# Infinity row of a Winograd-style dynamic convolution taken by direct products from DRAM taps, with the first softmax's transposes among them

## The chip, the cores and the metric

The kernel runs on one core of a Trainium2 chip. The metric is the device time of one execution in microseconds (us). Before the change three runs took 764.07, 766.85 and 767.55 us; the median is 766.85 us. The engines are called PE (matrix products), ACT (activations and copies), DVE (vector operations), POOL (vector operations and DMA descriptors) and SP (DMA issue). Each runs its own list of instructions in order, and they meet through semaphores.

## The reference

The input x is (4, 256, 64, 64) in float32: four images of 256 channels. Layer 0 makes, for each pixel, 49 attention weights, and sums the 49 shifted neighbours (7x7, dilation 2) with them. Layer 1 whitens the result over groups of 64 channels. Cut to what matters:

```python
k = lax.conv_general_dilated(x, w1, (1, 1), [(6, 6), (6, 6)], rhs_dilation=(2, 2), dimension_numbers=DN) + b1
k = lax.conv_general_dilated(k, w2, (1, 1), [(0, 0), (0, 0)], dimension_numbers=DN) + b2
attn = softmax(k, axis=1)                      # 49 weights per pixel
y = einsum('bkchw,bkhw->bchw', shifts, attn)   # 49 shifted copies of x
# layer 1, g = 4 groups of 64 channels, over all pixels of all images
Sigma = EPS * I + einsum('gdm,gem->gde', xc, xc) / m
# five Newton steps for Sigma^(-1/2), then xn = wm @ xc, times weight plus bias
```

## The kernel before

**Weights and points.** The two convolutions are folded at the start into one 7x7 convolution with 49 outputs, whose taps lie in `tap`. It is computed by evaluation and interpolation in both directions (Winograd's scheme): seven points 1, -1, 0, 2, -2, infinity (`INF`, number 6) and 1/2 for rows, and the same for columns. For a row point br, `row_eval` combines rows of x into `rb`, `col_ops` evaluates the columns into seven tiles `xh`, `conv_bank` multiplies them on PE with the weights `wr` in three banks (`BANKS`: three, three and one column points), ACT copies each bank from PSUM (`cv`) to `pv`, and `col_interp` turns a row's seven columns into `zz[:, br]` on DVE. When all rows are there, `row_interp` gives the logits. The row of infinity needs only the products of one row of taps (`taps(INF)` is `(0,)`), so it has half of a row's products.

**Direct products.** `direct` computes a row point without evaluating columns: 7 column taps v times 2 halves of channels times 2 halves of rows, each a product of up to 512 columns. It is used for image 0's rows infinity, 0, 4 and 5 (`direct0`) and, at the end of image 0's stage, for image 1's infinity, with the taps in SBUF and the result in `acc`.

**Stages.** Image 0 is computed with everything in a fixed order on DVE (`strict`). Then for b = 1, 2, 3 a list of steps `(cost, f)` is run: `conv_step` of each row in `ROWS`, which for images 2 and 3 begins with infinity. Each step also prepares (`prepare`: weights, row and column evaluation) the same bank of the next row. After each eighth of the costs a `gap` is filled with work of the image before: `soft` (softmax over 49, transposes on PE, exponentials on ACT), and for each quarter n of an image `first_half` and `second_half`, in which PE transposes blocks of x (`make_block`), multiplies them with a band matrix of the attention weights (`weighted_sum`), ACT stores y (`store_y`), and PE gathers the moments for layer 1 (`turn_y`, `moments`). The band matrix comes from softmax over DRAM: ACT copies terms into `zt` (`move_terms`), SP stores them to `sd` and loads them skewed into `band` in three parts, and DVE transposes the blocks (`load_band`).

**Weights over DRAM.** Row weights of points 4 and 5 and of infinity are kept in DRAM (`kept`: `g4d`, `g5d`, `gi`). When a row is first used after image 0, `weights` loads them into `rb[0]`, makes the bank's column weights on DVE and ACT, and stores them to `gd`; later images only load them. Two or three of the copies in it, `o0[0]`, `o1[0]` and `o0[INF]`, are plain copies on ACT (lines 405, 406 and 415).

**Slots.** The halves of an image lie in five slots. `move` stores slots 0 to 2 to DRAM when their image is finished and loads image 2's second half and image 3 there, by POOL's DMA queue.

**Buffers.** `pv` has `NV` = 3 buffers that rotate by row; the scratch tile of `col_interp` for b > 0 is the last point of the buffer after the next. `pivot`, a bias for y, is a DVE reduction behind image 0's stage (line 812).

Of the kernel before, what the change touches and what calls it, by code (L numbers as in the profile page):

```python
# [11 lines left out]
ALU = mybir.AluOpType  # L12
# [13 lines left out]
BANKS = ((1, 2, 0), (3, 4, 6), (5,))  # L26
ORDER = sum(BANKS, ())

ROWS = (INF, 0, 1, 2, 3, 4, 5)


@with_exitstack
def kernel(
# [222 lines left out]
    zz = apool.tile([P, NP, Q9, W], F32, name="zz")  # L256
    nc.gpsimd.memset(zz[:, INF], 0.0)

    NV = 3
    pv = apool.tile([P, NV, NP, Q9, 2 * Q9], F32, name="pv")  # L260
    ct = apool.tile([P, Q8 * 4 * Q8, 4], F32, name="ct")
    rb = [apool.tile([P, Q8, 2, NCC, W], F32, name=f"rb{k}") for k in range(3)]
    xh = {}
# [11 lines left out]

    TT, STT = nc.vector.tensor_tensor, nc.vector.scalar_tensor_tensor

    turn, strict = [None], [False]

    def in_turn(ins):  # L280


        if turn[0] is not None:
            tc.add_manual_dep(
                ins.ins,
                turn[0],
                mybir.DependencyInfo(mybir.DependencyClass.NoSync, mybir.DependencyReason.DATA),
                reason="in_turn",
            )
        if strict[0]:  # L290
            turn[0] = ins.ins.name
        return ins

    @contextmanager
# [66 lines left out]
    def weights(b, br, i, mid=None):  # L361

        first = (br, i) not in made
        made.add((br, i))
        s0 = slot_of[BANKS[i][0]]
        ns = sum(len(taps(bc)) for bc in BANKS[i])  # L370
        nk = NSK * len(taps(br)) // 2
        wt = apool.tile([P, ns, NSK], F32, tag=f"wr{i}", name=f"wr_{b}_{br}_{i}")[:, :, :nk]
        w = {bc: wt[:, slot_of[bc] - s0 : slot_of[bc] - s0 + len(taps(bc))] for bc in BANKS[i]}
        if not first:
            nc.sync.dma_start(wt, gd[br][:, s0 : s0 + ns])
            return w

        if br == 0:
            g = [gr0[:, v] for v in range(KS)]
        elif br in kept:  # L380

            f = rb[0].rearrange("p q r c w -> p (q r c w)")[:, : KS * nk]
            if i == 0:
                nc.sync.dma_start(f, kept[br])
            f = f.rearrange("p (v a r k) -> p v a r k", v=KS, a=NCC, k=KT)
            g = [f[:, v] for v in range(KS)]
        else:
            g = [gbr[:, v] for v in range(KS)]
        g = [t.rearrange("p a r k -> p (a r k)") for t in g]

        e = ct.rearrange("p a b -> p (a b)") if b else store[4].rearrange("p c r w -> p (c r w)")
        e, o, e1 = (e[:, k * nk : (k + 1) * nk] for k in range(3))
        g0 = [g[KS - 1 - a] for a in range(4)]
        g1 = [g[KS - 5 - a] for a in range(3)]
        o0 = {bc: w[bc][:, 0] for bc in w}
        o1 = {bc: w[bc][:, 1] for bc in w if bc != INF}
        if i == 0:
            add(e, g0[0], g0[2])
            add(o, g0[1], g0[3])
            add(e1, g1[0], g1[2])  # L400
            add(o0[1], e, o)
            sub(o0[2], e, o)
            add(o1[1], e1, g1[1])
            sub(o1[2], e1, g1[1])
            nc.scalar.copy(o0[0], g0[0])
            nc.scalar.copy(o1[0], g1[0])
        elif i == 1:
            madd(e, g0[2], 4.0, g0[0])
            madd(o, g0[3], 4.0, g0[1])
            madd(e1, g1[2], 4.0, g1[0])  # L410
            madd(o0[3], o, 2.0, e)
            madd(o0[4], o, -2.0, e)
            madd(o1[3], g1[1], 2.0, e1)
            madd(o1[4], g1[1], -2.0, e1)
            nc.scalar.copy(o0[INF], g0[3])
        else:
            madd(o0[5], g0[0], 2.0, g0[1])
            madd(o1[5], g1[0], 4.0, g1[2])
            madd(o0[5], o0[5], 2.0, g0[2])
            if mid is not None:  # L420
                mid()
            madd(o1[5], g1[1], 2.0, o1[5])
            madd(o0[5], o0[5], 2.0, g0[3])
            add(o1[5], o1[5], o1[5])
        for bc in BANKS[i]:
            f = SCALE[bc] * (SCALE[br] if br not in kept else 1.0)
            if f != 1.0:
                nc.scalar.mul(w[bc], w[bc], f)
        nc.sync.dma_start(gd[br][:, s0 : s0 + ns], wt)
        return w  # L430
# [82 lines left out]
    def conv_bank(b, br, i, w):  # L513

        if i == 0:
            slot[b, br] = len(slot) % NV
        pts = BANKS[i]
        i0 = sum(len(k) for k in BANKS[:i])
        cv = cv_buf[ncv[0] % 2][:, : 3 * PT].rearrange(
# [34 lines left out]
                    reason="later",  # L554
                )

    def interpolate(pt, tmp, outs, cut, part=None):

        lo = lambda t: cut(t, 0)
        hi = lambda t: cut(t, 1)
        c0, s1, s2, s3, s4, hh, c6 = (pt[b] for b in (0, 1, 2, 3, 4, 5, 6))
        if part != 1:
            add(tmp, s1, s2)
            sub(s2, s1, s2)  # L570
            add(s1, s3, s4)
            sub(s4, s3, s4)
            add(s3, c0, c6)
            madd(s1, tmp, -2.0, s1)
            sub(s3, tmp, s3)
            madd(tmp, tmp, -30.5, s1)
            sub(s4, s4, s2)
            madd(tmp, s3, 22.5, tmp)
            madd(s1, c0, 1.5, s1)
            madd(tmp, s2, -16.0, tmp)  # L580
            madd(s1, c6, -30.0, s1)
            if part is None:
                add(tmp, tmp, s4)
            madd(s3, s1, -1.0 / 6, s3)
            madd(outs[0], lo(s1), 1.0 / 6, hi(c0))
            if part == 0:
                add(outs[2], lo(c6), hi(s3))
                add(s3, tmp, s4)
        if part != 0:
            madd(hh, tmp if part is None else s3, -1.0 / 9, hh)  # L590
            if part is None:
                add(outs[2], lo(c6), hi(s3))
            madd(s4, hh, -3.0, s4)
            sub(s2, s2, hh)
            madd(s2, s4, -1.0 / 15, s2)
            madd(outs[1], lo(s4), 1.0 / 15, hi(s2))
# [5 lines left out]
    def col_interp(b, br, part=None):  # L602
# [6 lines left out]
        }  # L609
        outs = phases(zz[:K2, br].rearrange("p q (w two) -> p q w two", two=2))  # L610
        cut = lambda t, k: t[:, :, k : k + Q8]
        if b > 0:

            t = pv[:K2, (at + 2) % NV, NP - 1].rearrange("p q b -> p (q b)")
        else:
            t = ct.rearrange("p a b -> p (a b)")[:K2, :PT]
        interpolate(
            pt, t.rearrange("p (q b two) -> p q b two", q=Q9, two=2), outs, cut, part
        )

        def end():
            ins = nc.scalar.copy(outs[3], cut(pt[5], 0))
            if br == INF:

                nc.gpsimd.memset(zz[:, INF, Q8], 0.0)
            return ins

        if part is None and b > 0 and br != ROWS[-2]:
# [22 lines left out]

    logits = {}

    def direct(b, br, s, ps, w, xr=None):


        a = 3 if br == INF else 0
        order = [(v, cc) for v in sorted(range(KS), key=lambda v: abs(v - R)) for cc in range(NCC)]
        for j, (v, cc) in enumerate(order):
            d = 2 * (v - R)  # L660
            w0, w1_ = max(0, -d), min(W, W - d)
            for h in range(2):
# [22 lines left out]
    def conv_psum():  # L685
        ncv[0] += 1
        return cv_buf[(ncv[0] - 1) % 2].rearrange("p (q w) -> p q w", w=W)

    acc = ps_y.tile([P, 2, Q8, W], F32, tag="y", name="acc")
    nc.vector.memset(acc, 0.0)  # L690
    rows = [(0, br) for br in (1, 2, 3)]
    NR0 = len(rows)
    rows += [(b, br) for b in range(1, B) for br in ROWS[1 if b == 1 else 0 :]]
    cur, nxt = {}, {}

    def prepare(k, i):

# [3 lines left out]
            cur["x"] = row_eval(b, br)  # L701
        nxt.update(w)
        col_eval(cur["x"], i)

    def conv_step(k, i):
        w = {bc: nxt.pop(bc) for bc in BANKS[i]}
# [54 lines left out]
    for i in three:  # L761
        bank(0, i)
        both0(xr, 2, i)
    for s in range(2, 4):
        load_x(s, s, nc.gpsimd)
    for i in three:
# [16 lines left out]
    for sr in range(2):  # L783
# [14 lines left out]
    prepare(NR0, 0)  # L798
    direct0(5, 1)
    row_interp(0, 1)  # L800

    direct(1, INF, 0, acc[:, 0], [tap[:, UPOS[3], v] for v in range(KS)])
    prepare(NR0, 1)
    prepare(NR0, 2)
    strict[0] = False
    gpool.release()

    npix = SH * W // 4  # L810
    in_turn(
        nc.vector.tensor_reduce(
            pivot, slots[0].rearrange("p a r w -> p a (r w)")[:, :, :npix], AX.X, ALU.add
        )
    )
    nc.vector.tensor_scalar(pivot, pivot, -1.0 / npix, None, ALU.mult)

# [116 lines left out]

    BAND = ((0, 3), (3, 5), (5, 8))

    def load_band(n, part):

        if (n, part) in loaded or n not in moved:
# [4 lines left out]
        for g in range(CR):  # L946
# [5 lines left out]
                    ap=[[DW - 1, SW], [KS * SW, m1 - m0], [1, KS * SW]],  # L952
                ),
            )
        f = band[:, m0:m1].rearrange("p m r w -> p (m r w)")
        with tc.high_priority():
            nc.vector.transpose(f, f)  # L957
        if (n, part) == (4 * B - 1, len(BAND) - 1):
            bring_back(dma)

# [231 lines left out]
    for b in range(1, B):  # L1192

        steps = []
        for k, (bk, br) in enumerate(rows):
            if bk == b:
                for i, cost in enumerate((6, 5, 2)):
                    steps.append(
                        (cost * len(taps(br)) / 2, lambda k=k, i=i: conv_step(k, i))
                    )  # L1200
        if b == 1:
            steps.insert(0, (0, lambda: soft(0, 0)))
            steps.insert(4, (0, lambda: soft(0, 1)))
        j, at, whole = 0, 0, sum(c for c, _ in steps)
        for cost, f in steps:
            f()
            at += cost
            if at * NPC >= (j + 1) * whole:
                gap(b, j)
# [220 lines left out]
```

## Time and profile before

| what | value |
|---|---|
| median of three runs | 766.85 us |
| the profiled execution | 761.8 us, of it a span of 760.0 us |
| granted TensorE clock, mean | 0.978 |
| PE, products of the banks (L531) | 4576 records, 268.8 us |
| PE, direct products (L668), image 1's infinity and those to `acc` | 168 records of `acc<-slot,tap`, 34.6 us |
| DVE, interpolation on pv (L310, L306), two largest groups | 327 instructions, 98.4 us |
| DVE, transposes of band (L957) | 48 instructions, 50.9 us |
| ACT, evictions of banks (L541) | 69 instructions, 33.2 us, 101.8 us of waiting before them |
| POOL | 45 instructions, 33.7 us |

A product in float32 appears as two records. Busy time of PE is the time covered by records; durations on DVE overlap a little with the next instruction, so that the starts of two neighbours lie closer together than the duration says.

### The profile page before, as it was taken

The page shows a single profiled execution, that of the slowest core. Times are in us where ns is not written, and L with a number is a line of the kernel's source. Part 1 is how long each engine was busy: PE and PEld are TensorE (multiplying, and loading weights), DVE is VectorE, ACT ScalarE, POOL GpSimd, SP SyncE. Part 2 cuts the span into 40 slices and gives each one's busy share as a digit, 9 for nine tenths or more (in the row PEclk, how much of TensorE's full clock was granted, in tenths as well). Part 3 has the DMA queues.
Part 4 walks back from the last instruction along what each step waited for, and adds up shares of the span by engine and source line. Part 5 has one row for each costly group of instructions (what it writes and reads, how often), then busy time and mean ns, then how long its engine had stood idle before and what let it go on. Part 6 is the DMA issues. An engine that isn't in the chain of part 4 may idle for free.

```text
span 760.0 us, 18845 instructions
## 1 busy us (share of the span) xinstructions
PE 698.6 (92%) x7608; PEld 539.3 (71%) x7608; DVE 643.0 (85%) x1394; ACT 342.8 (45%) x980; POOL 33.7 (4%) x45
## 2 busy tenths in 40 slices
PE   6999999996999877999999977999999889998996
PEld 1459643376998766888998967998898668885322
DVE  3799899999999989999994999999979675545665
ACT  1414240255355726366545442745435473322464
POOL 0410000020000010002000100000000000000000
PEclk9999999999899989999999998999999999999999
DMA  8981120227163563246745731342532134363488
GB/s 323 254 293 72 60 86 0 87 98 233 33 220 120 198 216 88 80 141 217 226 137 184 233 105 47 126 111 91 165 90 79 50 98 140 117 232 136 191 357 338
DMA packets 62911, 115.39 MB, mean 152 GB/s; under 512 B 26295, under 2 KB 45416, under 8 KB 62056
## 3 DMA queue, kind: packets, MB, share of 16 engines
q1 hardware_dynamic: 59128, 95.31, 38.4%
q0 software_dynamic: 3696, 18.88, 7.2%
q8 instruction: 60, 0.98, 0.6%
q14 instruction: 27, 0.22, 0.1%
HBM read 66.18 MB, written 47.98 MB: 150 GB/s over the span
## 4 chain that ended last, share of the span: by engine, by line
DVE 44%; PE 41%; ACT 5%; DMA 4%; issue 4%; SPq 1%; DVEq 0%; ACTq 0%
PE cv L531 9%; PE y L1004 8%; PE acc L668 6%; DVE xh L310 6%; DVE pv L310 5%; DVE rb L310 4%; PE tp L1370 4%; DVE ct L310 3%; DVE band L957 3%; DVE ct L303 3%; DVE zz L310 3%; DVE pv L306 2%; PE tp L1036 2%; PE tp L975 2%; PE sig L1057 2%
## 5 line engine op out<-in xcount | busy, mean ns | idle before, releaser
L531 PE MATMUL cv<-xh,wr 128*49 128x128 f32 (+1 forms) x4576 | 268.8, 279 | 19.5 <-issue 7.3
L531 PEld LDWEIGHTS cv<-xh,wr 128*49 128x49 f32 x4576 | 260.6, 126 | 25.5 <-issue 18.0
L1004 PE MATMUL y<-band,xb 128*128 128x224 f32 (+2 forms) x640 | 151.2, 374 | 15.0 <-ACT xb L983 12.9
L1004 PEld LDWEIGHTS y<-band,xb 128*128 128x128 f32 x640 | 109.6, 193 | 36.4 <-ACT xb L983 16.0
L541 ACT COPY pv<-cv 113x486 f32<-113x486 f32 (+1 forms) x69 | 33.2, 483 | 101.8 <-PE cv L531 101.5
L1023 ACT ACTIVATE slot<-y,pivot 128x512 f32<-128x512 f32 x53 | 36.8, 741 | 62.1 <-PE y L1004 62.1
L310 DVE SCALAR_TENSOR_TENSOR pv<-pv 113x162 f32<-113x162 f32 x215 | 63.8, 318 | 0.5
L1044 ACT COPY yt<-tp 128x256 f32<-128x256 f32 x128 | 45.9, 379 | 36.3 <-PE tp L1036 35.2
L957 DVE STREAM_TRANSPOSE band<-band 128x960 f32<-128x960 f32 (+1 forms) x48 | 50.9, 1060 | 9.9 <-DMA band<-sd 9.9
L1036 PE MATMUL tp<-ident,slot 128*128 128x128 f32 x256 | 52.0, 299 | 4.4 <-ACT yt L1044 2.3
L975 PE MATMUL tp<-ident,slot 128*128 128x128 f32 x256 | 50.5, 300 | 4.6 <-ACT yt L1044 4.5
L1036 PEld LDWEIGHTS tp<-ident,slot 128*128 128x128 f32 x256 | 41.3, 205 | 13.3 <-issue 3.2
L975 PEld LDWEIGHTS tp<-ident,slot 128*128 128x128 f32 x256 | 40.4, 206 | 11.0 <-ACT yt L1044 6.0
L906 ACT COPY zt<-d 32x112 f32<-32x112 f32 (+2 forms) x156 | 45.0, 289 | 1.8
L860 ACT ACTIVATE d<-tp,mx 128x49 f32<-128x49 f32 x128 | 37.5, 335 | 14.0 <-DVE mx L855 10.7
L310 DVE SCALAR_TENSOR_TENSOR xh<-ct 128x512 f32<-128x512 f32 x46 | 30.3, 683 | 10.2 <-PE cv L531 10.2
L1057 PE MATMUL sig<-yt 128*64 128x65 f32 x1024 | 36.9, 225 | 0.0
L1057 PEld LDWEIGHTS sig<-yt 128*64 128x64 f32 x1024 | 32.5, 137 | 6.0 <-issue 4.5
L983 DVE COPY xb<-tp 128x256 f32<-128x256 f32 x41 | 16.4, 421 | 23.7 <-PE tp L975 23.7
L983 ACT COPY xb<-tp 128x256 f32<-128x256 f32 x87 | 30.4, 376 | 12.7 <-PE tp L975 12.0
L306 DVE TENSOR_TENSOR pv<-pv 113x162 f32<-113x162 f32 x112 | 34.6, 319 | 0.4
L668 PE MATMUL acc<-slot,tap 128*49 128x496 f32 (+3 forms) x168 | 34.6, 569 | 0.0
(221 smaller groups left out, 947.2 us busy)
## 6 DMA issues: line engine op xcount, KB each, us to landing
out_dram<-out SPq DMA_DIRECT2D x32, 512.0 KB, 3.4
sd<-zt SPq DMA_DIRECT2D x16, 896.0 KB, 4.2
slot<-in_x_dram POOLq DMA_DIRECT2D x12, 1024.0 KB, 9.2
band<-sd SPq DMA_DIRECT2D x128, 84.0 KB, 2.2
wr<-gd SPq DMA_DIRECT2D x15, 588.0 KB, 3.8
wr<-gd SPq DMA_DIRECT2D x15, 490.0 KB, 3.5
spill<-slot POOLq DMA_DIRECT2D x3, 2048.0 KB, 8.4
back<-spill SPq DMA_DIRECT2D x3, 2048.0 KB, 12.8
```

The source lines that it names most:

```text
L306: return in_turn(TT(o, a, b, ALU.subtract))
L310: return in_turn(STT(o, a, f, b, ALU.mult, ALU.add))
L531: nc.tensor.matmul(cv[h * HB : h * HB + KT, k, sr : sr + n, sc : sc + n], wv[:, sc, sr, cc], xh[bc][:, :n, h * NCC + cc, :n], start=(j == ...
L668: nc.tensor.matmul(ps[h * HB : h * HB + KT, :, w0:w1_], w[v][:, cc], xs[:, :, cc, w0 + d : w1_ + d], start=(j == 0), stop=(j == len(order) ...
L906: ins = nc.scalar.copy(o, i)
L957: nc.vector.transpose(f, f)
L975: nc.tensor.transpose(t[:, cc * P : (cc + 1) * P], xt[:, cc, CR * m : CR * (m + 1), bass.ds(pc, SW, 2)], ident,)
L983: (nc.vector.tensor_copy if tail else nc.scalar.copy)(xb, t[:, :C])
L1004: nc.tensor.matmul(ps[:, cc, q0 - half * HALF : q1 - half * HALF, :], xb[:, cc * P : (cc + 1) * P], rhs, start=(k == 0), stop=(k == len(PI ...
L1036: nc.tensor.transpose(t[:, cc * P : (cc + 1) * P], yt[:, cc, CR * i : CR * (i + 1), bass.ds(pc, SW, 2)], ident,)
L1044: nc.scalar.copy(yb.rearrange("p a g c -> p (a g) c")[:, :, :GW], t[:, :C].rearrange("p (e c) -> p e c", c=GW),)
L1057: nc.tensor.matmul(sig[g * GW : (g + 1) * GW, cc], yb[:, cc, g, :GW], yb[:, cc, g], start=(count[0] == 0 and cc == 0), stop=(count[0] == 4 ...
```

## The change

Infinity is no longer in `ROWS`. `direct_inf` computes it for images 1, 2 and 3 by direct products: it loads the taps of infinity from DRAM (`gi`) into `spare`, the first 686 elements of pv's third buffer, and puts the result through a `cv` buffer into `zz[:, INF]`. For image 1 it is the first step of its stage instead of the last of image 0's, and softmax's first call (`soft(0, 0)`) is made inside it, after six of the 14 pairs of a column tap and a half of the channels (`j == KS - 1`). For images 2 and 3 it is a step of cost 12.

Further: image 0 still rotates over three pv buffers and images 1 to 3 over two; the scratch tile of `col_interp` lies behind the taps in `spare`; `col_interp` makes its first four additions as two of double width (`pairs`); the plain copies of weights go to POOL for b > 0 (`same`); `pivot` is made by two ACT instructions with an accumulator during image 0; the transposes of band leave out the three rows of padding at both ends, and those of the first quarter (n = 0) are held and placed behind the preparation of the next row (`held`, `turn_blocks`).

```diff
...
-ROWS = (INF, 0, 1, 2, 3, 4, 5)
+ROWS = (0, 1, 2, 3, 4, 5)
...
     NV = 3
     pv = apool.tile([P, NV, NP, Q9, 2 * Q9], F32, name="pv")
+    NTAP = KS * NCC * KT
+    spare = pv[:, NV - 1].rearrange("p n q b -> p (n q b)")
     ct = apool.tile([P, Q8 * 4 * Q8, 4], F32, name="ct")
...
-    turn, strict = [None], [False]
+    turn, strict, latest = [None], [False], [None]
...
             )
+        latest[0] = ins.ins.name
         if strict[0]:
-            turn[0] = ins.ins.name
+            turn[0] = latest[0]
         return ins
...
         o1 = {bc: w[bc][:, 1] for bc in w if bc != INF}
+        same = nc.scalar.copy if b == 0 else nc.gpsimd.tensor_copy
         if i == 0:
...
             sub(o1[2], e1, g1[1])
-            nc.scalar.copy(o0[0], g0[0])
-            nc.scalar.copy(o1[0], g1[0])
+            same(o0[0], g0[0])
+            same(o1[0], g1[0])
         elif i == 1:
...
             madd(o1[4], g1[1], -2.0, e1)
-            nc.scalar.copy(o0[INF], g0[3])
+            same(o0[INF], g0[3])
         else:
...
         if i == 0:
-            slot[b, br] = len(slot) % NV
+            slot[b, br] = len(slot) % NV if b == 0 else (len(slot) - NV) % 2
         pts = BANKS[i]
...
-    def interpolate(pt, tmp, outs, cut, part=None):
+    def interpolate(pt, tmp, outs, cut, part=None, pairs=None):
...
         c0, s1, s2, s3, s4, hh, c6 = (pt[b] for b in (0, 1, 2, 3, 4, 5, 6))
+        both = tmp
+        if pairs is not None:
+            tmp, s1 = tmp[:, 0], tmp[:, 1]
         if part != 1:
-            add(tmp, s1, s2)
-            sub(s2, s1, s2)
-            add(s1, s3, s4)
-            sub(s4, s3, s4)
+            if pairs is not None:
+                add(both, *pairs)
+                sub(pairs[1], *pairs)
+            else:
+                add(tmp, s1, s2)
+                sub(s2, s1, s2)
+                add(s1, s3, s4)
+                sub(s4, s3, s4)
             add(s3, c0, c6)
...
         cut = lambda t, k: t[:, :, k : k + Q8]
-        if b > 0:
-            t = pv[:K2, (at + 2) % NV, NP - 1].rearrange("p q b -> p (q b)")
-        else:
-            t = ct.rearrange("p a b -> p (a b)")[:K2, :PT]
-        interpolate(
-            pt, t.rearrange("p (q b two) -> p q b two", q=Q9, two=2), outs, cut, part
-        )
+        t = ct.rearrange("p a b -> p (a b)") if b == 0 else spare[:, NTAP:]
+        t = t[:K2, : 2 * PT].rearrange("p (n q b two) -> p n q b two", q=Q9, two=2, n=2)
+        pair = lambda i: pv[:K2, at, i : i + 4 : 3].rearrange(
+            "p n q b -> p n (q b)"
+        ).rearrange("p n (q b two) -> p n q b two", q=Q9, two=2)
+        interpolate(pt, t, outs, cut, part, (pair(0), pair(1)))
...
             ins = nc.scalar.copy(outs[3], cut(pt[5], 0))
-            if br == INF:
-                nc.gpsimd.memset(zz[:, INF, Q8], 0.0)
             return ins
...
-    def direct(b, br, s, ps, w, xr=None):
+    def direct(b, br, s, ps, w, xr=None, mid=None):
...
         for j, (v, cc) in enumerate(order):
+            if j == KS - 1 and mid is not None:
+                mid()
             d = 2 * (v - R)
...
+    def direct_inf(b, mid=None):
+        nc.sync.dma_start(spare[:, :NTAP], kept[INF])
+        t = spare[:, :NTAP].rearrange("p (v a k) -> p v a k", v=KS, a=NCC)
+        direct(b, INF, 0, conv_psum(), [t[:, v] for v in range(KS)], mid=mid)
     acc = ps_y.tile([P, 2, Q8, W], F32, tag="y", name="acc")
...
     NR0 = len(rows)
-    rows += [(b, br) for b in range(1, B) for br in ROWS[1 if b == 1 else 0 :]]
-    cur, nxt = {}, {}
+    rows += [(b, br) for b in range(1, B) for br in ROWS]
+    cur, nxt, prepared = {}, {}, [None]
...
         col_eval(cur["x"], i)
+        prepared[0] = latest[0]
...
         both0(xr, 2, i)
+    npix = SH * W // 4
+    for cc in range(NCC):
+        nc.scalar.activation(
+            store[4].rearrange("p c r w -> p (c r w)")[:, SH * W : SH * W + npix],
+            slots[0][:, cc].rearrange("p r w -> p (r w)")[:, :npix],
+            AF.Identity, scale=-1.0 / npix, accum_out=pivot[:, cc : cc + 1],
+        )
     for s in range(2, 4):
...
     row_interp(0, 1)
-    direct(1, INF, 0, acc[:, 0], [tap[:, UPOS[3], v] for v in range(KS)])
     prepare(NR0, 1)
...
     gpool.release()
-    npix = SH * W // 4
-    in_turn(
-        nc.vector.tensor_reduce(
-            pivot, slots[0].rearrange("p a r w -> p a (r w)")[:, :, :npix], AX.X, ALU.add
-        )
-    )
-    nc.vector.tensor_scalar(pivot, pivot, -1.0 / npix, None, ALU.mult)
...
+    held = []
     def load_band(n, part):
...
             )
-        f = band[:, m0:m1].rearrange("p m r w -> p (m r w)")
-        with tc.high_priority():
-            nc.vector.transpose(f, f)
+        def turn_blocks(after=None):
+            f = band.rearrange("p m r w -> p (m r) w")[
+                :, m0 * BP + (R if m0 == 0 else 0) : m1 * BP - (R if m1 == NCH else 0)
+            ].rearrange("p e w -> p (e w)")
+            with tc.high_priority():
+                ins = nc.vector.transpose(f, f)
+            if after is not None:
+                tc.add_manual_dep(
+                    ins.ins,
+                    after,
+                    mybir.DependencyInfo(
+                        mybir.DependencyClass.NoSync, mybir.DependencyReason.DATA
+                    ),
+                    reason="turn_blocks",
+                )
+        if n == 0:
+            held.append(turn_blocks)
+        else:
+            turn_blocks()
         if (n, part) == (4 * B - 1, len(BAND) - 1):
...
                 for i, cost in enumerate((6, 5, 2)):
-                    steps.append(
-                        (cost * len(taps(br)) / 2, lambda k=k, i=i: conv_step(k, i))
-                    )
+                    steps.append((cost, lambda k=k, i=i: conv_step(k, i)))
         if b == 1:
-            steps.insert(0, (0, lambda: soft(0, 0)))
+            steps.insert(0, (0, lambda: direct_inf(1, lambda: soft(0, 0))))
             steps.insert(4, (0, lambda: soft(0, 1)))
+        else:
+            steps.insert(0, (12, lambda b=b: direct_inf(b)))
         j, at, whole = 0, 0, sum(c for c, _ in steps)
...
             f()
+            if held and at + cost == 13:
+                for g in held:
+                    g(prepared[0])
+                held.clear()
             at += cost
```

## The prediction

> **What bounds the kernel now.** I began with the page: the busy shares and the shares of the last chain.
>
> ```profile
> PE 698.6 (92%) x7608; PEld 539.3 (71%) x7608; DVE 643.0 (85%) x1394; ACT 342.8 (45%) x980; POOL 33.7 (4%) x45
> DVE 44%; PE 41%; ACT 5%; DMA 4%; issue 4%; SPq 1%; DVEq 0%; ACTq 0%
> ```
>
> No engine bounds the whole span; the chain is split between DVE and PE. So I asked for busy time by stage, with bounds at the places where the work changes hands (busy of PE, PEld, DVE, ACT, POOL; then the granted clock, DMA share, GB/s):
>
> ```profile
> 123.00:157.00 34.00, 34.00 (x169) 10.93 (x166) 33.09 (x73) 5.85 (x13) 1.68 (x1) 1.00 0.18 64
> 157.00:261.50 104.50, 92.90 (x1302) 86.33 (x1304) 103.38 (x236) 55.17 (x187) 7.23 (x8) 0.97 0.46 143
> 261.50:297.00 35.50, 29.67 (x342) 26.48 (x338) 31.91 (x75) 17.77 (x44) 3.38 (x2) 0.90 0.55 179
> 297.00:330.60 33.60, 29.24 (x404) 27.28 (x404) 33.41 (x68) 15.40 (x57) 0.00 (x0) 0.95 0.33 90
> 330.60:447.20 116.60, 113.17 (x1515) 103.11 (x1510) 104.61 (x231) 63.47 (x187) 8.03 (x7) 1.00 0.59 188
> 447.20:468.00 20.80, 12.90 (x191) 12.12 (x192) 20.52 (x42) 4.67 (x10) 0.00 (x0) 0.84 0.26 76
> 468.00:585.50 117.50, 114.63 (x1594) 105.79 (x1591) 111.83 (x240) 61.18 (x204) 0.15 (x1) 1.00 0.38 112
> ```
>
> DVE is full from 123 to 261.5 and again in 297-330.6 and 447-468; there PE has idle time (11.6, 4.4 and 7.9 us). In 330.6-447 and 468-585 it is PE that is full. The long gaps of PE, from its timeline (start, length; in brackets the idle time before, and what ended it):
>
> ```profile
> 145.34 11.55 PE L668 MATMUL acc<-slot,tap 128*49 128x512 f32 x56
> 172.68 11.80 PE L531 MATMUL cv<-xh,wr 128*49 128x128 f32 x208 [1.79 <-ACT pv L541]
> 189.88 7.75 PE L531 MATMUL cv<-xh,wr 128*49 128x128 f32 x96 [5.39 <-DVE xh L303]
> 277.62 1.17 PE L1004 MATMUL y<-band,xb 128*128 128x96 f32 x4 [4.32 <-ACT xb L983]
> 303.48 4.12 PE L531 MATMUL cv<-xh,wr 128*49 128x128 f32 x40 [3.55 <-DVE xh L310]
> 460.68 8.08 PE L531 MATMUL cv<-xh,wr 128*49 128x128 f32 x112 [7.34 <-issue]
> ```
>
> The gap before 277.62 has its cause on ACT, in front of the xb copy, and DVE then stands for the band that comes late:
>
> ```profile
> 276.85 0.27 ACT L405 COPY wr<-rb 128x98 f32<-128x98 f32 x1 [5.10 <-DMA rb<-gi]
> 282.94 1.18 DVE L957 STREAM_TRANSPOSE band<-band 128x960 f32<-128x960 f32 x1 [3.52 <-DMA band<-sd]
> ```
>
> ACT runs in order: the copy of an infinity weight waits 5.1 us for gi, and PE's next weighted sum waits behind it.
>
> **Infinity by tap columns (images 2 and 3).** On PE a row has 208 records in 11.80 us (56.7 ns each), an infinity row 104: 5.9 us. A direct product has 56 records in 11.55 us. So PE gains 5.65 us of work twice, **+11.3 us**. DVE loses, per image, the column evaluation (ct 1.22 twice, xh 0.68 seven times; started back to back they are 1.13 and 0.60 apart: 6.5 us) and the column interpolation (22 operations of some 0.32, 0.24-0.26 apart: 5.6 us). Image 2 also loses the making of the infinity weights: 20 operations on 128x98, 0.17 apart, 3.4 us. That is 15.5 + 12.1 us of DVE. ACT loses three evictions, two rb and two xh copies (5 us) and gains one zz copy (0.58), all in its idle 55%.
>
> In place of infinity, row 0 is now the row prepared during the last row of the image before. What counts is PE's time from the start of infinity to the end of row 0's first bank. Before, 297.06 to 314.66 is 17.6 us in image 2 and 447.23 to 468.69 is 21.5 us in image 3, because inside them lie gaps of 3.55, 0.71, 0.56 and 7.34 us that wait for xh of these very rows. After: 11.6 + 5.4 = 17.0 us each, with row 0's xh ready, since DVE no longer has the infinity row in between: **-0.6 and -4.5 us**.
>
> The slow products behind the gaps are in these sums. After 5.39, 3.55 and 7.34 us of idle, 96, 40 and 112 records took 2.3, 1.85 and 1.7 us longer than at 56.7 ns each. [...]
>
> **Taps from DRAM, image 1's too.** The product keeps its place in PE's order (145 us) and its length. Each product has one more DMA of 343 KB on SP. The compiled order puts image 2's load right behind image 1's, and image 3's into image 2's stage, so each waits only for the product before it, tens of us ahead of its use. Behind the second load in SP's queue stands the first sd store (172.1 us before), which needs softmax; behind the third stands a weight load for row (2,1). Neither is due earlier than the product's end: 0. The nearest load (wr<-gd, 588 KB) lands in 3.8 us; if one were late it would cost PE that, once per image, so 0 to 8, taken 0.
>
> **Copies to POOL, gi off ACT's path.** Image 1's nine copies of 128x196 leave ACT (0.36 each). The nearest POOL row is 0.24 for 128x64, so about 0.4 each. They are queued behind slot 4's load (171.6 us) and in front of the first spill (259 us): nothing on the path. [...] By the trace nothing can be said for copies: beside POOL's memsets at 157-162 us DVE's additions kept their 1.22. I take 0.5, with ends 0 and 3.6.
>
> The gi wait goes altogether: its weights aren't made. Then the half at 268-279 ends 4.3 us sooner, its band load starts sooner, and DVE's 3.52 us go too. What is late next is xh of row (1,5)'s last bank (before at 285.2), bound by DVE, and slot 0's reload (POOL, 268-281 us), for which ACT's first copies of image 2 wait at about the same time. So not 4.3 but **-4.0 us** in 261-297.
>
> **DVE in 123-261.** Here PE waits for DVE, so what DVE loses is gained: pivot on ACT (1.21 + 0.16: 1.4 us; in image 0's stage ACT is half idle); pairs of additions in one operation of 324. From 0.318 at 162 elements and 0.751 at 576 the slope is 1.05 ns, so two pairs save 0.35 us where each waits for the last (image 0, three rows) and 0.15-0.25 elsewhere: 1.1 + 1.0 us; shorter band transposes (96 of 960 elements: 0.1 us each, some seven here); half of the 0.9 us in which DVE waits for DMAs, as image 0's transposes now stand behind the next row's evaluation. Sum **-4.5 us**. Softmax's transposes amid the products reach PE at 145.3 + 5.1 = 150.4 us; the logits are complete at 151.6 (before), about a us earlier with the pairs. They cost PE 0 to 1.1 us, and let softmax start 5 us earlier; that gives order, no DVE time: 0.
>
> **Elsewhere.** In 314-330 the clock's and gaps' 1.2 us partly go: -0.6. In 330-447 and 468-600 PE idles 3.4 and some 5 us in short waits for ACT and DVE; with DVE now having slack, a third goes: -0.7 and -1.5. Pairs and transposes there save DVE another 5 us beside a full PE: 0. The tail after 600 is as before.
>
> **Sum:** -4.5 -4.0 -0.6 -0.6 -0.7 -4.5 -1.5 = -16.4, with +0.5 for POOL and +0.5 for the transposes' wait: **-15.4 us**. The profiled execution is 760.0 span in 761.8 us; it becomes about 746.4. The median shown, 766.85, is 5 us above that execution; from it, **751.4 us**.
>
> **Rivals.**
>
> - *PE doesn't fill its gaps* (17%). For: slot 0's reload lands at about 281 and slot 2's at about 432 whatever DVE does, and ACT stands in order behind them; short waits for xb are not DVE's. Against: in 447-468 DVE is full with the infinity row's own work. Then 261-297 gives nothing, 447-468 half, the rest 0: -4.5 - 0.6 - 2.2 + 1 = -6: 761 (to 766 if the 123-261 part is also half).
> - *More* (10%): PE's idle in 123-600 is 38 us; if all but 2% goes, 38 - 9 + 4 of clock - 11.3 = -22: 745.
> - *Slower* (8%): column buffers. pv's third buffer is now the taps' and scratch space, so images 1 to 3 rotate over two. ACT's eviction of row r+1's first bank must wait until DVE has interpolated row r-1; ACT stands in order, and PE's next bank and xb behind it. Against: before, row (1,1) was interpolated by 203 us and row (1,3) evicted at 223.9, a margin of 21 us. It decides once DVE falls back by more than this; at 1.5 us for each of 17 rows it is +25, and with the rest 776.
> - *The change doesn't do what it says*: the order shows transposes amid products and no infinity row; what may fail is only the overlap, 1 us.
>
> The forecast (-21 to -8) has 65%. A measurement of this kernel tells no less than about 0.5% (3.8 us) from no change. Faster: 65 + 10 + 7 of the first rival = 82%; within: 10%; slower: 8%. Range 743 to 763: the larger gain below; above, the first rival up to its half.
>
> **What would show it.** L531's records fall from 4576 to 4368 and the direct line's gain 112; no wait for gi on ACT; DVE busy some 36 us less (27.6 infinity, 1.4 pivot, 4 to 5 pairs, 3 transposes); PE's gaps before 277.6, 303.5 and 460.7 gone, the clock near 1.00 in these stages; the direct products of images 2 and 3 at 11.6 us without a wait in front. Wrong if evictions (pv) wait for DVE, if PE waits at a direct product for taps or a slot, or if DVE's rows beside POOL's copies grow.

## The result and the profile after

The changed kernel takes 759.1 us (median of four executions, 756.5 to 760.0). The kernel before took 767.15 us over four executions. The ratio is 0.990, with a 95% interval of 0.986 to 0.994. So the change brings about 8 us, half of the 15.4 us forecast: faster by about 1%, and inside the range of 743 to 763 us, but far from the forecast. In what follows, executions more than 1.5% above the fastest of their kernel are left out of the ratios, but not out of the medians.

The busy shares and the shares of the last chain, from the page of the changed kernel:

```profile
PE 707.3 (93%) x7512; PEld 533.4 (70%) x7512; DVE 611.7 (81%) x1268; ACT 333.2 (44%) x953; POOL 62.8 (8%) x52
PE 65%; DVE 23%; ACT 5%; issue 3%; DMA 2%; SPq 1%; DVEq 0%; ACTq 0%
```

DVE lost 31.3 us of work and 126 instructions, and its share of the chain fell from 44% to 23%. PE gained 8.7 us. POOL's busy time rose by 29.1 us, for nine copies that were reckoned at 0.4 us each. That is the first sign.

The stages, by the view of busy time in windows (length; busy of PE, PEld, DVE, ACT, POOL; then clock, DMA share, GB/s):

```profile
257.30:303.80 46.50, 31.84 (x346) 28.55 (x340) 36.78 (x77) 16.68 (x38) 3.38 (x2) 0.82 0.58 191
303.80:336.50 32.70, 32.70 (x329) 23.46 (x328) 24.93 (x33) 17.27 (x67) 0.00 (x0) 1.00 0.23 75
450.60:471.00 20.40, 20.40 (x140) 11.49 (x142) 20.09 (x27) 7.09 (x17) 0.00 (x0) 1.00 0.04 11
471.00:582.30 111.30, 109.63 (x1595) 102.38 (x1592) 100.07 (x212) 56.98 (x192) 0.00 (x0) 1.00 0.38 118
```

The stage that took 35.5 us before (from 261.5 us, with a clock of 0.90) now takes 46.5 us at 0.82. The stages that begin with a direct product have no idle PE any more (32.70 of 32.70 us, 20.40 of 20.40) and a clock of 1.00. The change works where infinity was replaced, and loses what it gains there in one other place. Between fixed points of PE's order, in the two profiled executions:

| stretch | before, us | after, us | difference | forecast |
|---|---|---|---|---|
| start to row (1,4)'s last bank | 261.5 | 257.3 | -4.2 | -4.0 (-4.5, +0.5) |
| to image 2's infinity | 35.6 | 46.5 | **+10.9** | -3.5 (-4.0, +0.5) |
| to image 3's infinity | 150.2 | 146.7 | -3.4 | -1.9 |
| to the end of image 3's last bank | 137.8 | 131.5 | -6.3 | -6.0 |
| to the end | 175.0 | 176.2 | +1.2 | 0 |

The sum is -1.8 us, that of the two profiled executions. The one before (761.8 us) lies below all four timed runs of its kernel, the one after (760.0 us) is the highest of its four; the medians are 8 us apart. The traces can't place these other 6 us.

Now the bad stretch: PE's timeline (start, length; in brackets the idle time before, and what ended it).

```profile
257.33 3.72 PE L537 MATMUL cv<-xh,wr 128*49 128x128 f32 x64
268.25 6.10 PE L537 MATMUL cv<-xh,wr 128*49 128x128 f32 x64 [7.20 <-DVE xh L310]
...
279.73 4.70 PE L537 MATMUL cv<-xh,wr 128*49 128x128 f32 x80
291.63 3.66 PE L537 MATMUL cv<-xh,wr 128*49 128x128 f32 x32 [7.20 <-DVE xh L314]
```

The wait for gi and the gap of 4.32 us behind it are gone, as forecast, but PE stands twice for 7.2 us and waits for xh of row (1,5): once inside that row's first bank, with 32 of its 96 records done (the first line also holds the last 32 of row (1,4)), and once before its third bank. So the question is what DVE did, from its timeline:

```profile
253.98 1.22 DVE L307 TENSOR_TENSOR ct<-rb 128x1024 f32<-128x1024 f32 x1
255.23 0.72 DVE L307 TENSOR_TENSOR xh<-ct 128x512 f32<-128x512 f32 x1
266.77 0.85 DVE L978 STREAM_TRANSPOSE band<-band 128x640 f32<-128x640 f32 x1 [10.83 <-DMA band<-sd]
```

DVE stood 10.83 us for a load of band, with the next xh operation behind the transpose in its order. The load was late because of SP, whose queue shows:

```profile
247.33 0.32 SPq L964 DMA_DIRECT2D band<-sd  x1
256.19 0.32 SPq L435 DMA_DIRECT2D gd<-wr  x1
256.60 7.29 SPq L964 DMA_DIRECT2D band<-sd  x7
```

For 8.5 us SP issued nothing: seven loads of band stood behind the store of row (1,5)'s first bank of weights, which waited for its data. In the kernel before, the same store came 2.2 us behind the load ahead of it:

```profile
250.74 0.32 SPq L947 DMA_DIRECT2D band<-sd  x1
253.30 0.32 SPq L429 DMA_DIRECT2D gd<-wr  x1
253.71 5.29 SPq L947 DMA_DIRECT2D band<-sd  x7
```

In the changed kernel the data come in part from POOL:

```profile
97.17 13.99 POOL L411 COPY wr<-lgx 128x196 f32<-128x196 f32 x1 [52.02 <-ACT lgx L811]
...
225.91 0.80 POOL L411 COPY wr<-rb 128x196 f32<-128x196 f32 x1 [52.06 <-DMA rb<-g4d]
...
244.16 11.25 POOL L411 COPY wr<-rb 128x196 f32<-128x196 f32 x1 [15.94 <-DMA rb<-g5d]
255.35 0.81 POOL L412 COPY wr<-rb 128x196 f32<-128x196 f32 x1
```

The same copy of 128x196 takes 0.8 us for row (1,4), 13.99 us for row (1,0) and 11.25 us for row (1,5). SP's queue agrees with the last of these spans: the bank's second copy ends at 256.16 us and the store is issued at 256.19. The copy for row (1,0) was hidden; that for row (1,5) starts the chain POOL, SP, band, DVE, PE.

### The profile page after: what moved, and what is told of

Read it like the earlier page. It is cut to its first block, busy times and chain, and to the rows that moved or that the text cites. A ratio compares the mean times of both kernels' runs of the same rounds, so it can differ in the third digit from the quotient of the medians.

```text
span 758.2 us, 18491 instructions
## 1 busy us (share of the span) xinstructions
PE 707.3 (93%) x7512; PEld 533.4 (70%) x7512; DVE 611.7 (81%) x1268; ACT 333.2 (44%) x953; POOL 62.8 (8%) x52
## 4 chain that ended last, share of the span: by engine, by line
PE 65%; DVE 23%; ACT 5%; issue 3%; DMA 2%; SPq 1%; DVEq 0%; ACTq 0%
PE cv L537 22%; PE y L1039 13%; PE acc L679 6%; PE tp L1410 4%; PE tp L1071 4%; PE sig L1092 4%; PE tp L1010 3%; PE cv L679 3%; DVE zz L314 2%; DVE xh L314 2%; DVE ct L314 2%; DVE pv L314 2%; DVE zz L310 2%; DVE band L978 2%; DVE zz L307 2%
## 5 line engine op out<-in xcount | busy, mean ns | idle before, releaser
L537 PE MATMUL cv<-xh,wr 128*49 128x128 f32 x4368 | 254.0, 278 | 19.0 <-DVE xh L310 7.2
L537 PEld LDWEIGHTS cv<-xh,wr 128*49 128x49 f32 x4368 | 247.5, 125 | 23.7 <-issue 10.3
L547 ACT COPY pv<-cv 113x486 f32<-113x486 f32 (+1 forms) x63 | 30.0, 475 | 90.1 <-PE cv L537 84.8
L978 DVE STREAM_TRANSPOSE band<-band 128x864 f32<-128x864 f32 (+1 forms) x48 | 47.5, 992 | 13.5 <-DMA band<-sd 13.5
L314 DVE SCALAR_TENSOR_TENSOR pv<-pv 113x162 f32<-113x162 f32 x186 | 54.8, 318 | 1.8 <-ACT pv L547 1.1
L314 DVE SCALAR_TENSOR_TENSOR xh<-ct 128x512 f32<-128x512 f32 x42 | 27.9, 682 | 14.0 <-PE cv L537 13.7
L679 PE MATMUL cv<-slot,pv 128*49 128x496 f32 (+3 forms) x168 | 34.9, 571 | 0.0
L434 ACT ACTIVATE wr<-wr 128x392 f32<-128x392 f32 (+1 forms) x36 | 17.5, 513 | 33.5 <-DVE wr L307 16.5
```

Source lines behind the costliest of these rows:

```text
L314: return in_turn(STT(o, a, f, b, ALU.mult, ALU.add))
L537: nc.tensor.matmul(cv[h * HB : h * HB + KT, k, sr : sr + n, sc : sc + n], wv[:, sc, sr, cc], xh[bc][:, :n, h * NCC + cc, :n], start=(j == ...
L679: nc.tensor.matmul(ps[h * HB : h * HB + KT, :, w0:w1_], w[v][:, cc], xs[:, :, cc, w0 + d : w1_ + d], start=(j == 0), stop=(j == len(order) ...
L978: ins = nc.vector.transpose(f, f)
```

## The experiments

The last column is the time from the start of row (1,4)'s last bank to the start of image 2's infinity on PE, in the profiled execution.

| kernel | median, us | ratio to before, 95% interval | stretch, us |
|---|---|---|---|
| before | 764.81 to 766.65 in the three timed sets of runs | | 35.6 |
| changed | 759.1 | 0.986 to 0.994 | 46.5 |
| e1_act: copies on ACT | 750.59 | 0.974 to 0.984 | 38.1 |
| e2_dve: copies on DVE | 748.56 | 0.973 to 0.981 | 37.4 |
| e3_before_pool: before, copies on POOL | 764.84 | 0.997 to 1.002 | 36.0 |
| e4_store: POOL issues the gd stores | 751.74 | 0.977 to 0.986 | 39.0 |
| e5_act_prio: e1, third bank first | 747.81 | 0.975 to 0.983 | 32.6 |
| e6_dve_prio: e2, third bank first | **745.95** | 0.973 to 0.978 | 33.1 |
| e7_one_input: one more copy on DVE | 759.07 | 0.988 to 0.993 | 46.1 |
| e8_inf_rows: e1, infinity as rows | 757.47 | 0.987 to 0.993 | 38.4 |
| e9_no_pairs: e1, no pairs, pivot on DVE | 751.84 | 0.976 to 0.988 | 38.5 |
| e10_row5: two copies on ACT | 751.63 | 0.975 to 0.986 | 38.4 |
| e11_break: two additions, with a break | 761.1 (one execution) | | 38.2 |
| e12_nobreak: two additions, without | 762.45 (one execution) | | 45.7 |

**The copies off POOL.** e1_act and e2_dve change one line of the changed kernel:

```diff
-        same = nc.scalar.copy if b == 0 else nc.gpsimd.tensor_copy
+        same = nc.scalar.copy                                  # e1_act
+        same = nc.scalar.copy if b == 0 else (lambda o, i: in_turn(nc.vector.tensor_copy(o, i)))  # e2_dve
```

> The changed kernel with all plain copies of weights on ACT, as before; the rest as changed. Theory (POOL's copy of row (1,5)'s first bank takes 11.25 us beside a full DVE; SP's store of that bank stands behind it and seven loads of band behind the store; DVE waits 10.8 us for band and PE twice 7.2 us for xh): the copy is below 1 us, PE's two gaps of 7.2 us before row (1,5)'s second and third bank go, the stretch from row (1,4)'s last bank to image 2's infinity (46.5 us in the changed kernel) falls by 9 to 14 us, and the time from 759 to 746 to 751 us. Rival A (these gaps belong to DVE's own work and to the slots' reload, the copy only fills idle time): the gaps stay within 2 us and the time is 757 to 761 us.

> The changed kernel with the plain copies of weights of images 1 to 3 on DVE, in its order. Theory: as with the copies on ACT, PE's two gaps go; DVE has nine copies more of some 0.27 us (2.4 us) in 220 to 300 us, where it is full, so 748 to 753 us, 0 to 3 us behind the copies on ACT, unless these wait on ACT for g5d (some 2 us). Rival A: 757 to 763 us.

Both times fall as the theory said, by 8.5 and 10.5 us (8.0 and 9.7 by the ratios), and rival A is out. (The first gap, which the expectation puts before the second bank, lies inside the first.) One part of the expectation failed: in e1_act the stretch shrinks by 8.4 us only, the first gap is gone, and PE still waits 8.36 us before the third bank. So the copy isn't the whole story. (e1_act's profiled execution was some 10 us late already by 160 us; only the length of its stretch is read.)

**Which copy, and by which way.** e10_row5 takes two of the nine copies off POOL; e4_store leaves all of them there and takes the stores out of SP's queue.

```diff
+        same = nc.scalar.copy if b == 0 or (br, i) == (5, 0) else nc.gpsimd.tensor_copy   # e10_row5
...
-        nc.sync.dma_start(gd[br][:, s0 : s0 + ns], wt)
+        (nc.sync if b == 0 else nc.gpsimd).dma_start(gd[br][:, s0 : s0 + ns], wt)         # e4_store
```

> The changed kernel with only the two plain copies of row (1,5)'s first bank on ACT; the other seven of image 1 stay on POOL, among them the one of 13.99 us in image 0's stage. Theory (this one copy, at this place in front of SP's band loads, is the whole cost of the copies): as with all copies on ACT, 748 to 752 us, and the copy of 13 to 14 us in image 0's stage still there and hidden. Rival (the copies' cost is spread over POOL's other copies, DVE's slower operations beside them or the ACT time): 754 to 758 us.

> The changed kernel, copies still on POOL, but the stores of new weights of images 1 to 3 to gd are issued by POOL instead of SP, so that no load of band is queued behind a store that waits for the copy. If the harm goes through SP's queue: the copy stays slow (8 to 12 us), DVE's wait of 10.8 us for band falls below 3 us and the time is 747 to 752 us. If the harm is the late weights themselves (row (1,5)'s first bank can't start before its copy): a gap of 4 to 8 us stays in front of that row and the time is 752 to 757 us. Rival A: 757 to 761 us.

e10_row5 gives what e1_act gives. Its POOL timeline shows that the slowness went on to the next copy:

```profile
224.51 0.37 POOL L411 COPY wr<-rb 128x196 f32<-128x196 f32 x1 [50.69 <-DMA rb<-g4d]
...
246.07 9.31 POOL L421 COPY wr<-rb 128x196 f32<-128x196 f32 x1 [19.68 <-PE cv L537]
```

9.31 us for the second bank's copy cost nothing, since no load of band waits behind that bank's store; the first bank's store now comes 1.1 us behind the load ahead of it (247.63 and 248.72 us). In e4_store row (1,5)'s first copy still takes 9.34 us, but SP issues eight loads of band at 248.72 us, DVE's wait of 10.8 us for band is gone (a later one of 3.5 us stays), and the time falls to 751.74 us. Both say the same: the cost isn't the slow copy but what stands behind it in SP's queue.

**The copies on POOL in the kernel before.**

> The kernel before with only the plain copies of weights moved to POOL for images 1 to 3. Theory: row (1,5)'s first copy on POOL takes 5 to 14 us here too[...]; store and band loads come late and the stage grows by 4 to 12 us, while the copies of infinity no longer hold ACT for gi (about 4 us back): 765 to 775 us. Rival B (the slow copy comes from something else in the change, such as the held transposes or another order of SP): the copies take below 1 us and the time is 760 to 764 us, as the forecast took it.

No change of time (764.84 against 765.57 us), between both expectations. Here row (1,5)'s first copy began just behind a place where DVE idled (0.42 us) and took 0.36 us; the third took 3.18 us, an infinity copy 2.77 us, and that of image 0's stage 13.82 us. So slow copies come with POOL, not with the rest of the change, and which of them is hit differs from trace to trace.

The run shows a second thing, which bears on the forecast's -4.0 us. ACT no longer stands for gi here, and the gap of 4.32 us in front of the weighted sum is gone. Yet the stretch is as long as before, 36.0 against 35.6 us, because PE then waits for xh in front of row (1,5)'s third bank, whose last operation stands on DVE behind a transpose that waits for band (PE's line, then DVE's):

```profile
288.49 3.66 PE L532 MATMUL cv<-xh,wr 128*49 128x128 f32 x32 [6.27 <-DVE xh L310]
286.08 1.18 DVE L958 STREAM_TRANSPOSE band<-band 128x960 f32<-128x960 f32 x1 [3.29 <-DMA band<-sd]
```

**The second gap: DVE's order.** In e10_row5, PE's timeline shows what is left of the stretch:

```profile
257.47 7.27 PE L537 MATMUL cv<-xh,wr 128*49 128x128 f32 x128
...
283.90 3.66 PE L537 MATMUL cv<-xh,wr 128*49 128x128 f32 x32 [9.08 <-DVE xh L314]
```

The three xh operations of row (1,5)'s third bank lie on DVE at 280.4, 282.1 and 283.1 us, behind the row interpolation (14 operations of 0.74 us from 264.0 to 275.1 us, with others between them) and behind a transpose that waits 3.12 us for band:

```profile
278.21 1.08 DVE L978 STREAM_TRANSPOSE band<-band 128x864 f32<-128x864 f32 x1 [3.12 <-DMA band<-sd]
...
283.07 0.68 DVE L314 SCALAR_TENSOR_TENSOR xh<-xh,rb 128x512 f32<-128x512 f32 x1
```

In the kernel before, two of the three lay inside the row interpolation; the third stood behind such a transpose too. e5_act_prio and e6_dve_prio give this preparation priority:

```diff
+        last = i == len(BANKS) - 1 and b > 0 and br == ROWS[-2]
         if k + 1 < len(rows):
-            prepare(k + 1, i)
+            with tc.high_priority() if last else nullcontext():
+                prepare(k + 1, i)
...
-            last = br == ROWS[-2]
```

> The changed kernel with the copies on ACT and the preparation of row (1,5)'s third bank (and of the same bank in images 2 and 3) given priority over the interpolation of rows. With the copies on ACT alone PE still waited 8.4 us for xh of this bank, whose three operations the compiled order had put behind the row interpolation and a transpose of band. Theory (a second cause of the missing gain is this order of DVE): the gap of 8.4 us falls below 2 us, image 2's infinity starts 5 to 8 us earlier and the time is 742 to 747 us against 750.6. Rival C (DVE has as much to do before that point in either order, the gap only moves to the row interpolation or the next band): 749 to 752 us.

> The same priority with the copies on DVE. There the compiled order already has two of the three operations inside the row interpolation and the gap is 2.2 us. Theory of the order: at most 2 us to gain, 745 to 748 us against 748.6. Rival C: 748 to 751 us.

The gap is gone in both, and the stretch is 5.5 and 4.3 us shorter. The time gains less, 2.8 and 2.6 us, with ratios whose intervals overlap those of e1_act and e2_dve: in e5_act_prio the gap goes and another of 3.44 us for xb appears, and to image 3's infinity both take longer (148.3 against 146.7 us, 148.9 against 146.9). e5_act_prio ends just above its expectation, e6_dve_prio inside it and as the fastest of all. The gap that is left in e6_dve_prio's stretch waits for a copy of xb on ACT, from its timeline of PE:

```profile
269.91 2.50 PE L1040 MATMUL y<-band,xb 128*128 128x320 f32 x4 [4.37 <-ACT xb L1019]
...
288.81 11.59 PE L679 MATMUL cv<-slot,pv 128*49 128x512 f32 x56
```

On ACT this copy stands behind a scaling of row weights that waits 1.80 us for DVE, so DVE is in this gap too; what would take it away wasn't tried.

**What makes a copy slow.** e7_one_input puts a copy of 128x196 on DVE behind the weights of each first bank.

> The changed kernel, copies on POOL, with one more operation on DVE: a copy of 128x196 (one input) behind the weights of each first bank of images 1 to 3, into scratch. In the runs so far every slow POOL copy ends where DVE has its first break or its first operation with one input. Theory (a POOL copy gets no turn while DVE starts two-input operations back to back): row (1,5)'s copy, 11.25 us, now ends at this copy, after 3 to 5 us; the copy of 13.99 us in image 0's stage, which DVE's extra copy doesn't meet, stays above 13 us; the wait for band goes and the time is 749 to 754 us. Rival D ([...]a copy is slow in proportion to DVE's load): 10 to 11 us, and 758 to 760 us.

The theory in this form fell: 10.44 us, and 759.07 us, as rival D had it. (The trace is of the longest of 20 executions, 764.1 us; four of the others took 750.6 to 754.1 us, and no trace shows what differed in them.) But reading the starts against the lengths on DVE gave a better one. Beside this copy each operation of DVE starts some 0.08 us before the one ahead of it ends; so does the one behind the extra copy (252.51 + 0.24 = 252.75, next start 252.68). In the changed kernel the first exception after 244.16 us is in the fence of DVE above: 253.98 + 1.22 = 255.20, and the next, which reads what was just written, starts at 255.23. The slow copy ends 0.2 us later. e11_break and e12_nobreak test this in image 0's stage, where DVE's order is fixed, with two additions behind `row_weights(5)`:

```diff
+    add(cf[:, :196], g4[:, :196], g4[:, :196])
+    add(cf[:, 196:392], cf[:, :196], cf[:, :196])      # e11_break
+    add(cf[:, 196:392], g4[:, :196], g4[:, :196])      # e12_nobreak, in its place
```

> The changed kernel with two additions of 128x196 more on DVE in image 0's stage, where DVE's order is fixed, behind the row weights of point 5 (after 103.2 us), into scratch; the second reads what the first wrote, so that DVE must stop between them. In the runs so far the slow POOL copies end some 0.2 us after the first place where an operation of DVE starts later than the one before it ended. Theory (DVE's unbroken run keeps POOL out, and such a break lets it in): the POOL copy of image 0's stage, 13.8 to 14.0 us in every run, ends at these additions, after 6 to 7 us; DVE's rows show the break. If the copy's length is a matter of load: 13.5 to 14.5 us. The time is the changed kernel's, 756 to 761 us, since that copy is hidden.

> The same two additions, but both read the weights, so that neither waits for the other. Theory: no break, and the copy takes as long as without them plus their 0.5 us, 14 to 15 us. If any two additional operations of this kind let POOL in: 6 to 7 us, as with the dependent ones. The time is 756 to 761 us.

DVE's and then POOL's timeline of e11_break:

```profile
102.59 0.87 DVE L307 TENSOR_TENSOR gb<-gb 128x686 f32<-128x686 f32 x1
103.38 0.37 DVE L307 TENSOR_TENSOR ct<-gbr 128x196 f32<-128x196 f32 x1
103.78 0.38 DVE L307 TENSOR_TENSOR ct<-ct 128x196 f32<-128x196 f32 x1
```

```profile
97.32 6.63 POOL L411 COPY wr<-lgx 128x196 f32<-128x196 f32 x1 [52.90 <-ACT lgx L815]
...
226.92 14.03 POOL L411 COPY wr<-rb 128x196 f32<-128x196 f32 x1 [52.91 <-DMA rb<-g4d]
...
250.77 0.42 POOL L411 COPY wr<-rb 128x196 f32<-128x196 f32 x1 [9.23 <-DMA band<-sd]
```

And in e12_nobreak, DVE's timeline at the additions (the second line), then POOL's:

```profile
106.47 0.88 DVE L307 TENSOR_TENSOR gb<-gb 128x686 f32<-128x686 f32 x1
107.25 0.64 DVE L307 TENSOR_TENSOR ct<-gbr 128x196 f32<-128x196 f32 x2
107.80 1.30 DVE L314 SCALAR_TENSOR_TENSOR slot<-slot 128x512 f32<-128x512 f32 x2
```

```profile
101.20 14.54 POOL L411 COPY wr<-lgx 128x196 f32<-128x196 f32 x1 [56.12 <-DMA gd<-wr]
```

Behind the one break of 0.03 us (103.38 + 0.37 = 103.75, next start 103.78) the copy ends, at 103.95, after 6.63 us; the same additions without it leave 14.54 us. So in this pair, of one execution each, the copy with the break was 7.9 us shorter, and nearly all the other slow copies end 0.2 us behind a break too (last section). That speaks against rival D: DVE's load is the same in both. In e11_break another copy was then hit, row (1,4)'s with 14.03 us. It ended 0.2 us after DVE ran dry at 240.75 us, and the chain came one row earlier: the store behind it was issued at 241.27 us, DVE stood 7.86 us for band, and row (1,4)'s last bank started at 266.6 instead of 257.3 us. Row (1,5)'s copy took 0.42 us, and the stretch behind it, 38.2 us, is that of e1_act, with no edit there. The execution took 761.1 us; e12_nobreak's took 762.45 us, 1.5 us over its expectation. One execution can't tell these from 759.

**The sizes of two terms.**

> The changed kernel with the copies on ACT and infinity of images 2 and 3 again as rows with evaluated columns; image 1's stays direct from DRAM. It sizes the infinity part of the forecast (in 297 to 330 and 447 to 468: 0.6 + 0.6 + 4.5, and the wait for gi, some 4, with it; 1 to 3 more in 330 to 600 where DVE gets slack). By the forecast's terms: 10 to 13 us slower than with direct products, 760 to 764 us. Rival (PE's 11.3 us more of products eat what the gaps give): within 3 us of 750.6.

> The changed kernel with the copies on ACT, without pairs in the column interpolation and with pivot as a DVE reduction behind image 0's stage, as before. It sizes two of the terms in 123 to 261: by the forecast 1.4 (pivot) + 1.1 + 1.0 (pairs) = 3.5 us up to the end of the first image's second quarter, nothing beside a full PE later: 752 to 756 us against 750.6. Rival (this stage's gain comes from the shorter and held transposes and from image 1's taps, so that pairs and pivot give below 1 us): 749 to 752 us. Here the order of DVE differs too: two of the three operations of row (1,5)'s third bank lie inside the row interpolation again, which can give 1 to 3 us back after 261; so the two are to be read from the place where row (1,4)'s last bank starts.

e8_inf_rows is 6.9 us slower than e1_act, where 10 to 13 were reckoned. PE's gaps in the infinity rows are back (2.92 us in image 2, 7.25 us in image 3), but the stretch in front of image 2's infinity is as long as in e1_act (38.4 against 38.1 us): ACT waits for gi again, 6.33 us, but PE doesn't wait for ACT there. e9_no_pairs reaches row (1,4)'s last bank at 257.9 us, among the 257.1 to 258.2 us of e8_inf_rows, the changed kernel, e10_row5 and e4_store, which all have pairs and the new pivot. Its median lies in its rival's range, 1.2 us above e1_act's, with intervals that overlap. So the trace shows nothing of the 3.5 us that were reckoned up to there; what pairs and pivot are worth, if anything, is lost in the scatter of 1 us.

## Why the prediction was wrong

- **The step that failed most** is the cost of the copies on POOL: 0.4 us each from the row of 128x64, "nothing on the path", +0.5 in all with ends 0 and 3.6 (nine times 0.4). One took 11.25 us, and it was on the path. The 0.5 was the author's estimate, and it was put on the wrong engine: DVE's rows grew little (`rb<-slot` of 128x512 from 0.68 to 0.83 us beside copies of 0.8 us), while on POOL copies of one size took from 0.34 to 14.54 us, and the long ones ended, all but one, 0.2 us after a break of DVE. Naming what stood behind it would have needed SP: the prediction looked at POOL's queue for slot loads and spills, but not at the store that waits for the copy, with seven loads of band behind it. Price: 8.4 us of the stretch (46.5 to 38.1) and 8.5 us of the median.
- **-4.0 for the wait for gi** failed too, by itself: without the wait, and with nothing of the change but the copies on POOL, the stretch stays at 36.0 us (e3_before_pool), and in the changed kernel with the copies off POOL it is still 2.5 us longer than before. That "DVE's 3.52 us go too" is what didn't come: DVE waits for band as long as before, 3.29 us in e3_before_pool and 3.12 us in e10_row5; what holds those loads wasn't tested. The prediction named what is late next, xh of row (1,5)'s third bank, but priced it at 0.3 us. With two copies on ACT (e10_row5) PE is ready for that bank at 274.8 us, 11 us earlier than before (279.57 + 8.24 less 32 records of 56.7 ns: 286.0), but DVE's last xh operation ends only 1.5 us earlier (283.8 against 285.3), since the compiled order puts these operations last, behind that wait. With that order mended, the stretch is 2.4 to 2.9 us shorter than before, so the remaining error is 1.1 to 1.6 us.
- **-4.5 in 123 to 261** came out as -4.2, but by luck as to its terms: of the 3.5 put on pairs and pivot, e9_no_pairs shows nothing clear of scatter. The shorter and held transposes and the earlier softmax weren't undone one by one, so what gave the rest stays open.
- **-0.6, -0.6, -0.7, -4.5, -1.5** for the stretches that begin with infinity: -3.4 and -6.3 against -1.9 and -6.0. The gaps before 303.5 and 460.7 went, the clock is 1.00, and nothing waits for taps or slots. Bank records fell from 4576 to 4368 as reckoned; DVE lost 31.3 us of work against 36. (One of the gaps in these sums, 0.71 us, was ended by ACT's copy of a bank, not by xh.)
- **Column buffers**, the slower rival: one eviction in image 3, at 548.40 us, is listed as released by DVE after 5.03 us of idle time, but PE finished its bank only at 548.36 us, so it cost nothing; no other appeared.
- **The end**, taken as unchanged, was 1.2 us longer. In the traces of the experiments it runs from 173.3 to 176.6 us (before: 175.0), so this is within their scatter.

With the copies off POOL the changed kernel takes 750.6 to 751.6 us, near the 751.4 us of the forecast, but in part by luck. The stretch in front of image 2's infinity is then still some 6 us longer than forecast, and those behind it are 2 us shorter. And e10_row5's profiled execution (751.2 us) is only 10.6 us shorter than the one before (761.8 us), not 15.4; the rest of the difference of the medians is in no trace.

## What to carry to other kernels

When work moves to an idle engine, price it by the company it will keep there, and ask which queue issues something that waits for it and what stands behind that: here a copy reckoned at 0.4 us took 11.25 us and held a store, and the store held the loads for which the critical engine stood 10.83 us. When a wait is removed, the next late thing must get a time of its own, not only a name, and that means reading the compiled order, since a scheduler may put exactly that thing last.

## What the runs showed of the hardware

The shortest POOL copies of 128x196 in float32 took 0.34 to 0.44 us. Beside DVE operations that start before the one ahead ends such a copy took 9.3 to 14.5 us twelve times in seven of the traces, and eleven of these ended 0.2 us after the first break in DVE's run, which was as short as 0.03 us (e12_nobreak). In e7_one_input a one-input copy on DVE (0.24 us) stood beside a POOL copy of 10.44 us, which went on for 6.3 us after it; the twelfth long copy, 9.34 us in e4_store, ended during a transpose on DVE (0.83 us), without a break. In other places a copy took 0.8 us without any break, with DVE's operations beside it at 0.83 us instead of 0.68: what decides between the two stays open.
